# Softmax denominators from node blocks added on VectorE, and feed-forward blocks spread over the attention quads, in a two-layer graph kernel

## The chip, the cores and the metric

One core of one Trainium2 chip. The metric is the device time of one execution in microseconds (us), the median of several runs on the same chip. A trace of one execution accompanies every kernel. The engines are TensorE (PE in the profile, its weight loads PEld), VectorE (DVE), ScalarE (ACT), GpSimd (POOL) and the sync engine (SP).

## The reference, cut to what matters

64 graphs of 256 nodes with 256 features pass a graph attention layer (two attentions, a feed-forward block of width 1024) and then a relational attention layer with 8 heads of 32 features and 4 relations. The adjacency is 0 or 1, so only relations 0 and 1 occur. The change is in the second layer's attention:

```python
scores = jnp.einsum('bhid,bhjd->bhij', q, k) / np.sqrt(dh)
attn = jax.nn.softmax(scores, axis=-1)
out = jnp.zeros_like(q)
for r in range(Wv.shape[0]):
    v_r = (src @ Wv[r] + bv[r]).reshape(Bb, Nn, h, dh).transpose(0, 2, 1, 3)
    mask = (adj_matrix == r)[:, None]
    out = out + jnp.einsum('bhij,bhjd->bhid', attn * mask, v_r)
```

## The kernel before

Everything is float32. Graphs go two at a time (a group; 32 groups). A turn of the software pipeline works on three groups at once: the second layer of group `y_`, the rest of the first layer of `x_ = y_ + 1`, and the first attention of `z = y_ + 2`. TensorE's order is fixed by hand, to the order in which the code issues its instructions. The last turns, 30 and 31, lack a `z`, and turn 31 lacks an `x_` too.

The attention of a group is four quads: graph `b` (2) by half of the heads `m` (2, four heads each). `weighted` computes the transposed scores, their exponentials `e` (no maximum is subtracted; a check at the end guards this) and `ea = e * adjacency`. `applied` sums over the source nodes, which lie on the partitions in two blocks `j` of 128: `zo`, the denominators, by products with ones; `po`, the numerators, by products with the values (relation 0 for all, the difference of relations 1 and 0 where the adjacency is 1). Each head has 32 output columns, so four heads lie beside each other in TensorE as column tiles (128*32 in the trace). `divided` ends a graph. (`P` is 128, `N` 256, `NB` 2, `HPB` 4, `DH` 32, `F` 256.)

```python
    def weighted(u, b, m, q, k_, aT):
        ...                                  # scores: 8 products into four of six rotating PSUM banks
        for a in range(HPB):
            nc.scalar.activation(e[:, a, :], ps[a], AF.Exp, scale=isd)
        for a in range(0, HPB, 2):
            nc.vector.tensor_tensor(ea[:, a:a + 2, :], e[:, a:a + 2, :],
                                    ab[:, None, :].to_broadcast([P, 2, NB * N]), ALU.mult)
        return e, ea

    def applied(b, m, v, e, ea, po, zo):
        terms = [(zo, lambda h, j: ones, e), (po, lambda h, j: v[:, b * NB + j, h * DH:(h + 1) * DH], e),
                 (po, lambda h, j: v[:, b * NB + j, F + h * DH:F + (h + 1) * DH], ea)]
        for n, (to, lhs, rhs) in enumerate(terms):
            for j in range(NB):
                for a in range(HPB):
                    hp = slice(a * DH, (a + 1) * DH)
                    nc.tensor.matmul(to[hp, m * N:(m + 1) * N], lhs(m * HPB + a, j),
                                     rhs[:, a, j * N:(j + 1) * N],
                                     start=(n < 2 and j == 0), stop=(n != 1 and j == NB - 1))

    def divided(u, b, po, zo, oT):
        rz = work.tile([P, KB * N], F32, tag="rz", name=f"rz{u}_{b}")
        nc.vector.reciprocal(rz, zo)
        nc.gpsimd.tensor_add(low, low, rz)
        nc.vector.tensor_tensor(oT[...], po..., rz..., ALU.mult)
    ...
    def turn(y_, x_, z):
        ...                                  # values, queries, keys; then the attention stretch:
            e = {0: weighted(y_, *quads[0], q, k_, aT)}
        ...
            h1 = hidden(x_, 0, h1hT, wf1, bf1, AF.Relu, range(FB // 2))
        ...
            e[1] = weighted(y_, *quads[1], q, k_, aT)
            apply_(0)
            e[2] = weighted(y_, *quads[2], q, k_, aT)
            apply_(1)
            e[3] = weighted(y_, *quads[3], q, k_, aT)
        ...
            hidden(x_, 0, h1hT, wf1, bf1, AF.Relu, range(FB // 2, FB), h1)
        ...
            early(z)                         # transposes of adjacency (aTp) and input (xT)
        ...
            apply_(2)
            apply_(3)
        ...                                  # out_(0), project(z), out_(1): yop, xpp, yop
```

## Time and profile before

| | before |
|---|---|
| median of 3 runs | 3420.71 us (3419.79 to 3422.26) |
| TensorE, VectorE, ScalarE, GpSimd busy | 98%, 49%, 32%, 29% |
| granted TensorE clock, mean | 0.991 |
| steady turn (first aTp to the next first aTp) | 103.64 us |

A busy share says which engine to look at, not what an instruction costs. In this document a stretch of TensorE lasts from the first start of one group of instructions to the first start of the next group, because the lengths given for matmuls overlap (rows of 1.05 us start 0.86 us apart). The prediction shows the lines.

### The profile page before, as it was taken

What the parts mean: (1) busy time and instruction counts of PE and PEld (TensorE: products, weight loads), DVE (VectorE), ACT (ScalarE), POOL (GpSimd) and SP (SyncE); (2) the same over time, 40 slices, a digit from 0 to 9 for tenths busy, and PEclk for the clock granted to TensorE, in tenths of its full rate; (3) what the DMA queues carried; (4) which work ended last, traced back from release to release, by engine and by line L of the source; (5) the groups of instructions that cost most, each with busy time, mean ns of one, the idle gap of its engine ahead of it and who ended that gap; (6) DMA issues with size and microseconds to landing.
All of it is one profiled execution on the core that took longest, in us unless ns stands there. A gap on an engine that the chain in (4) does not pass through costs nothing.

```text
span 3419.7 us, 45212 instructions
## 1 busy us (share of the span) xinstructions
PE 3341.6 (98%) x18970; PEld 2199.3 (64%) x18970; DVE 1683.3 (49%) x3479; ACT 1079.6 (32%) x1920; POOL 983.7 (29%) x844
## 2 busy tenths in 40 slices
PE   4899999999999999999999999999999999999997
PEld 3566666666666666666666666676666666666664
DVE  2545555444554444554454554454544445554544
ACT  1333323323323323333333333233233233333222
POOL 1233232332322332322332323322323323223312
PEclk8999999999999999999999999999999999999998
DMA  4000000000000000000000000000000000000000
GB/s 122 17 15 14 13 19 19 13 19 7 19 19 19 13 19 7 19 19 19 13 19 7 20 19 13 19 10 16 20 19 13 19 7 20 19 19 7 7 1 14
DMA packets 62465, 61.04 MB, mean 18 GB/s; under 512 B 7216, under 2 KB 61616, under 8 KB 62256
## 3 DMA queue, kind: packets, MB, share of 16 engines
q1 hardware_dynamic: 33792, 33.56, 3.0%
q0 software_dynamic: 16896, 16.78, 2.1%
q10 hardware_dynamic: 11568, 7.76, 0.9%
q8 instruction: 151, 2.47, 0.3%
q14 instruction: 58, 0.48, 0.0%
HBM read 41.31 MB, written 16.78 MB: 17 GB/s over the span
## 4 chain that ended last, share of the span: by engine, by line
PE 97%; DVE 1%; DMA 1%; ACTq 0%; POOL 0%; issue 0%; ACT 0%; POOLq 0%; DVEq 0%
PE h1p L655 26%; PE yfp L617 26%; PE vp L687 6%; PE po L723 6%; PE sp L703 4%; PE zo L723 4%; PE hpp L606 3%; PE yop L617 3%; PE kp L674 3%; PE qp L674 3%; PE ygp L617 3%; PE xpp L568 3%; PE rows L578 1%; PE aTp L555 1%; DMA b<-in_L_gnn_b_dram 0%; ACTq L462 0%
## 5 line engine op out<-in xcount | busy, mean ns | idle before, releaser
L655 PE MATMUL h1p<-h1T,wf 128*128 128x512 f32 x1024 | 457.5, 600 | 0.1
L711 DVE TENSOR_TENSOR ea<-e,aT 128x1024 f32<-128x1024 f32 x256 | 317.9, 1283 | 272.7 <-ACT e L709 272.7
L655 PE MATMUL h1p<-h3T,w 128*128 128x512 f32 x1024 | 446.5, 594 | 1.4 <-DVE h3T L544 1.4
L617 PE MATMUL yfp<-wf,h 128*128 128x256 f32 x2048 | 447.3, 379 | 0.0
L617 PE MATMUL yfp<-w,h 128*128 128x256 f32 x2048 | 447.3, 379 | 0.0
L617 PEld LDWEIGHTS yfp<-w,h 128*128 128x128 f32 x2048 | 386.8, 190 | 52.2 <-issue 1.0
L617 PEld LDWEIGHTS yfp<-wf,h 128*128 128x128 f32 x2048 | 386.7, 190 | 51.3
L709 ACT ACTIVATE e<-sp 128x512 f32<-128x512 f32 x512 | 264.2, 604 | 380.3 <-PE sp L703 380.3
L655 PEld LDWEIGHTS h1p<-h3T,w 128*128 128x128 f32 x1024 | 194.8, 191 | 234.3 <-issue 229.4
L655 PEld LDWEIGHTS h1p<-h1T,wf 128*128 128x128 f32 x1024 | 189.8, 190 | 236.5 <-issue 217.8
L730 POOL TENSOR_TENSOR low<-low,rz 128x512 f32<-128x512 f32 x64 | 81.1, 1268 | 852.4 <-DVE rz L729 852.4
L587 DVE SCALAR_TENSOR_TENSOR s<-s 128x512 f32<-128x512 f32 x128 | 90.3, 706 | 443.0 <-ACT s L584 441.8
L645 POOL TENSOR_TENSOR res<-res,rb 128x1024 f32<-128x1024 f32 x128 | 301.1, 2352 | 10.0
L620 DVE TENSOR_TENSOR yf<-yfp,res 128x512 f32<-128x512 f32 x128 | 88.5, 692 | 424.7 <-PE yfp L617 423.4
L633 POOL TENSOR_TENSOR rs<-ve,mhalf 128x4 f32<-128x4 f32 x128 | 130.6, 1020 | 456.5 <-DVE ve L632 456.5
L657 ACT ACTIVATE h<-h1p,b 128x512 f32<-128x512 f32 x256 | 175.8, 687 | 250.7 <-PE h1p L655 249.4
L729 DVE RECIPROCAL rz<-zo 128x512 f32<-128x512 f32 x64 | 214.7, 3354 | 67.5 <-PE zo L723 67.5
L657 ACT ACTIVATE h<-h1p,bf 128x512 f32<-128x512 f32 x256 | 176.9, 691 | 213.9 <-PE h1p L655 213.9
L687 PE MATMUL vp<-wv,h2T 128*128 128x512 f32 x512 | 230.1, 592 | 0.0
L676 ACT ACTIVATE q<-qp,bq 128x512 f32<-128x512 f32 x64 | 44.0, 687 | 530.6 <-PE qp L674 530.6
L608 ACT COPY hp<-hpp 128x258 f32<-128x258 f32 x128 | 47.9, 374 | 442.5 <-PE hpp L606 442.5
L644 POOL TENSOR_TENSOR res<-yf,rg 128x1024 f32<-128x1024 f32 x64 | 150.5, 2351 | 95.8 <-DVE yf L637 94.3
(485 smaller groups left out, 4319.7 us busy)
## 6 DMA issues: line engine op xcount, KB each, us to landing
xs<-in_x_dram SPq DMA_DIRECT2D x32, 512.0 KB, 3.8
af<-in_adj_dram POOLq DMA_DIRECT2D x32, 512.0 KB, 4.4
out_dram<-res SPq DMA_DIRECT2D x32, 512.0 KB, 2.9
wf<-in_L_gnn_w_ff_dram ACTq DMA_DIRECT2D x2, 1024.0 KB, 11.5
w<-in_L_gnn_W_dram ACTq DMA_DIRECT2D x2, 1024.0 KB, 10.0
wv<-in_L_gnn_Wv_dram ACTq DMA_DIRECT2D x2, 256.0 KB, 4.6
gw<-in_L_gnn_W_dram ACTq DMA_DIRECT2D x1, 256.0 KB, 4.5
gw2e<-in_L_gnn_W_dram ACTq DMA_DIRECT2D x1, 256.0 KB, 6.9
```

The lines of the kernel that those rows point to most:

```text
L617: nc.tensor.matmul(ps[:, i * F:(i + 1) * F], lhs(t, k), rhs(b, k), start=(k == 0), stop=(k == n - 1))
L644: nc.gpsimd.tensor_mul(r, xn, g[:, None, :].to_broadcast([P, T, F]))
L645: nc.gpsimd.tensor_add(r, r, b[:, None, :].to_broadcast([P, T, F]))
L655: nc.tensor.matmul(ps, wi[:, k, f * P:(f + 1) * P], hT[:, k, :], start=(k == 0), stop=(k == KB - 1))
L657: nc.scalar.activation(h1[:, f, :], ps, func, bias=bi[:, f:f + 1])
L674: nc.tensor.matmul(ps, w[:, k, m * P:(m + 1) * P], hT[:, k, :], start=(k == 0), stop=(k == KB - 1))
L687: nc.tensor.matmul(ps, hT[:, k, t * P:(t + 1) * P], wvf[:, k, :], start=(k == 0), stop=(k == KB - 1))
L703: nc.tensor.matmul(ps[a][:, j * N:(j + 1) * N], k_[hp, m, j0:j0 + P], q[hp, m, b * N:(b + 1) * N], start=True, stop=True)
L709: nc.scalar.activation(e[:, a, :], ps[a], AF.Exp, scale=isd)
L711: nc.vector.tensor_tensor(ea[:, a:a + 2, :], e[:, a:a + 2, :], ab[:, None, :].to_broadcast([P, 2, NB * N]), ALU.mult)
L723: nc.tensor.matmul(to[hp, m * N:(m + 1) * N], lhs(m * HPB + a, j), rhs[:, a, j * N:(j + 1) * N], start=(n < 2 and j == 0), stop=(n != 1 an ...
L729: nc.vector.reciprocal(rz, zo)
```

## The change

Its intent: TensorE is the bound, and half of the zo products only add two blocks of nodes. VectorE, half idle, can add the blocks, and then one product with ones a head is enough. The sums take VectorE time between the scores and the apply of a quad, so the eight hidden blocks of the other group's feed-forward are spread to give it that time. The diff, with cuts:

```diff
-        return e, ea
+        es = work.tile([P, HPB, N], F32, tag="es", name=f"es{n}")
+        nc.vector.tensor_add(es, e[:, :, 0:N], e[:, :, N:2 * N])
+        return e, ea, es
...
+        terms = [(j, v[:, b * NB + j, r * F + m * P:r * F + (m + 1) * P], w)
+                 for r, w in ((0, e), (1, ea)) for j in range(NB)]
+        for n, (j, vs, w) in enumerate(terms):
+            for a in range(HPB):
+                hp = slice(a * DH, (a + 1) * DH)
+                nc.tensor.matmul(po[hp, m * N:(m + 1) * N], vs[:, hp], w[:, a, j * N:(j + 1) * N],
+                                 start=(n == 0), stop=(n == len(terms) - 1))
+        for a in range(HPB):
+            nc.tensor.matmul(zo[a * DH:(a + 1) * DH, m * N:(m + 1) * N], ones, es[:, a, :],
+                             start=True, stop=True)
...
+            if have(y_):
+                yield scores, 0
+            yield hid, range(0, 3)
+            if have(y_):
+                yield scores, 1
+                yield apply_, 0
+            yield hid, range(3, 4)
+            if have(y_):
+                yield scores, 2
+                yield apply_, 1
+            yield hid, range(4, 6)
+            if have(y_):
+                yield scores, 3
+            yield hid, range(6, 8)
+            if have(z):
+                yield early, z
+            if have(y_):
+                yield apply_, 2
+                yield apply_, 3
```

Three things change, then: half of zo goes, four sums a turn come, and the hidden blocks stand at four places instead of two. A fourth: zo is now the last term of an apply, and was the first.

More of the change, by code (lines that the diff above doesn't have):

```diff
@@ L712, in weighted, with applied @@
                                     ab[:, None, :].to_broadcast([P, 2, NB * N]), ALU.mult)
-        return e, ea
-    def applied(b, m, v, e, ea, po, zo):
-        terms = [(zo, lambda h, j: ones, e), (po, lambda h, j: v[:, b * NB + j, h * DH:(h + 1) * DH], e),
-                 (po, lambda h, j: v[:, b * NB + j, F + h * DH:F + (h + 1) * DH], ea)]
-        for n, (to, lhs, rhs) in enumerate(terms):
-            for j in range(NB):
-                for a in range(HPB):
-                    hp = slice(a * DH, (a + 1) * DH)
-                    nc.tensor.matmul(to[hp, m * N:(m + 1) * N], lhs(m * HPB + a, j),
-                                     rhs[:, a, j * N:(j + 1) * N],
-                                     start=(n < 2 and j == 0), stop=(n != 1 and j == NB - 1))
+        es = work.tile([P, HPB, N], F32, tag="es", name=f"es{n}")
+        nc.vector.tensor_add(es, e[:, :, 0:N], e[:, :, N:2 * N])
+        return e, ea, es
+    def applied(b, m, v, e, ea, es, po, zo):
+        terms = [(j, v[:, b * NB + j, r * F + m * P:r * F + (m + 1) * P], w)
[8 more added lines that the diff above has]
+                             start=True, stop=True)
     def divided(u, b, po, zo, oT):
@@ L790, in turn, with scores @@
             acc = [None] * G
-            e = {0: weighted(y_, *quads[0], q, k_, aT)}
+            e = {}
+            def scores(n):
+                e[n] = weighted(y_, *quads[n], q, k_, aT)
             def apply_(n):
@@ L799, in apply_, with steps, hid @@
                     divided(y_, b, *acc[b], oT)
-        if have(x_):
-            h1 = hidden(x_, 0, h1hT, wf1, bf1, AF.Relu, range(FB // 2))
-        if have(y_):
-            e[1] = weighted(y_, *quads[1], q, k_, aT)
-            apply_(0)
-            e[2] = weighted(y_, *quads[2], q, k_, aT)
-            apply_(1)
-            e[3] = weighted(y_, *quads[3], q, k_, aT)
-        if have(x_):
-            hidden(x_, 0, h1hT, wf1, bf1, AF.Relu, range(FB // 2, FB), h1)
-        if have(z):
-            early(z)
-        if have(y_):
-            apply_(2)
-            apply_(3)
+        h1 = None
+        def steps():
+            if have(y_):
[17 more added lines that the diff above has]
+                yield apply_, 3
+        def hid(blocks):
+            nonlocal h1
+            if have(x_):
+                h1 = hidden(x_, 0, h1hT, wf1, bf1, AF.Relu, blocks, h1)
+        for do, what in steps():
+            do(what)
         if have(y_):
```

## The prediction

> **What bounds the kernel now.** I read the page's busy shares and slices first, then the chain that ended last, then the timeline of one turn of the software pipeline on TensorE, VectorE and ScalarE, and last the groups by shape.
>
> The page: busy time, the TensorE slices, the chain.
>
> ```profile
> PE 3341.6 (98%) x18970; PEld 2199.3 (64%) x18970; DVE 1683.3 (49%) x3479; ACT 1079.6 (32%) x1920; POOL 983.7 (29%) x844
> ...
> PE   4899999999999999999999999999999999999997
> ...
> PE 97%; DVE 1%; DMA 1%; ACTq 0%; POOL 0%; issue 0%; ACT 0%; POOLq 0%; DVEq 0%
> ```
>
> TensorE is busy 98% and the chain that ended last is TensorE for 97% of the span; only the first 5% and the last slice have holes. A microsecond off another engine is worth nothing unless TensorE waits for it. So the question is how many microseconds of TensorE issue go and come. A busy share cannot tell that (ends of matmuls are modelled, durations overlap), so I take differences of starts from the timeline of TensorE: start, length, engine, line, operation, tiles, count.
>
> ```profile
> 1545.42 13.90 PE L655 MATMUL h1p<-h3T,w 128*128 128x512 f32 x32
> 1559.15 0.60 PE L578 MATMUL rows<-ident,hp 128*128 128x128 f32 x4
> ...
> 1592.43 1.15 PE L703 MATMUL sp<-q,k 32*128 32x256 f32 x16
> 1593.51 7.13 PE L655 MATMUL h1p<-h1T,wf 128*128 128x512 f32 x16
> 1600.57 1.15 PE L703 MATMUL sp<-q,k 32*128 32x256 f32 x16
> 1601.65 1.07 PE L723 MATMUL zo<-e,ones 128*32 128x256 f32 x16
> 1602.54 1.05 PE L723 MATMUL po<-e,v 128*32 128x256 f32 x16
> 1603.40 1.05 PE L723 MATMUL po<-ea,v 128*32 128x256 f32 x16
> 1604.38 1.15 PE L703 MATMUL sp<-q,k 32*128 32x256 f32 x16
> ...
> 1609.26 7.13 PE L655 MATMUL h1p<-h1T,wf 128*128 128x512 f32 x16
> 1616.23 1.04 PE L555 MATMUL aTp<-ident,af 128*128 128x128 f32 x8
> ...
> 1622.41 1.05 PE L723 MATMUL po<-ea,v 128*32 128x256 f32 x16
> 1623.38 0.92 PE L617 MATMUL yop<-wo,oT 128*128 128x256 f32 x3
> ```
>
> No row has an idle time in brackets: in a steady turn TensorE waits for nobody. Turns repeat exactly; the first aTp of this turn starts at 1616.23 and that of the turn before at 1512.59, 103.64 us apart. Each product in the source is two instructions here (8 products in a zo term, 16 instructions).
>
> VectorE and ScalarE of the same turn show when their results are ready:
>
> ```profile
> 1594.71 2.36 DVE L711 TENSOR_TENSOR ea<-e,aT 128x1024 f32<-128x1024 f32 x2 [1.48 <-ACT e L709]
> 1602.85 2.36 DVE L711 TENSOR_TENSOR ea<-e,aT 128x1024 f32<-128x1024 f32 x2 [5.78 <-ACT e L709]
> 1606.65 2.36 DVE L711 TENSOR_TENSOR ea<-e,aT 128x1024 f32<-128x1024 f32 x2 [1.44 <-ACT e L709]
> 1608.93 3.35 DVE L729 RECIPROCAL rz<-zo 128x512 f32<-128x512 f32 x1
> 1612.39 0.69 DVE L731 TENSOR_TENSOR oT<-po,rz 128x512 f32<-128x512 f32 x1
> 1613.00 2.85 DVE L711 TENSOR_TENSOR ea<-e,aT 128x1024 f32<-128x1024 f32 x2
> ```
>
> VectorE waits for ScalarE's exponentials here, not the other way round. From 1592.4 to 1623.4 (the attention stretch, 31.0 us) it is busy 18.54 us, so it has room.
>
> [...] rows of 1.05 us start 0.86 us apart; hence starts only. [...] This kernel has three modes: full array (128*128), four row tiles (scores, 32*128), four column tiles (zo and po, 128*32). The plain rate of a full 512-column instruction is 13.73/32 = 0.429 us (h1p on h3T), so 16 take 6.87. Between two score groups 16 took 7.06 (1593.51 to 1600.57), between scores and transposes 6.97 (1609.26 to 1616.23): entering full from row mode costs 0.10, leaving it for row mode 0.09. A po term followed by po lasts 0.86; followed by scores 0.98, by yop 0.97: leaving column mode costs 0.11 to 0.12. [...] the same-sized ea products take 1222 ns in the stretch 1592 to 1610 (grouped by shape), 1283 over the run. [...] the ea pair of 2.85 us instead of 2.36 ran beside GpSimd's addition to low[...].
>
> **The change part by part.**
>
> (1) The zo term is halved. Before: 2 node blocks by 4 heads = 8 products a quad; after: 4, on e already added over the blocks. Four column tiles run together: 16 instructions start over 0.86 us (po) to 0.89 (zo, the term after scores), so 8 cost 0.43. Four quads a turn: 1.73 us; 32 turns: 55 us, all on TensorE and all on the path. That is 1.6% of 3421 at the very most.
>
> (2) The node blocks are added on VectorE: four more 128x1024 additions a turn, about 1.22 each by ea, 4.9 us; 128 of them are 156 us, VectorE rises from 1683 to some 1840 us (54%). In the attention stretch 18.5 becomes 23.4 of about 29.6 us. Off the path if no wait follows; checked under the clock below.
>
> (3) The hidden blocks, before as 4 behind scores 0 and 4 behind scores 3, become 3, 1, 2, 2. The products are the same, but two groups now stand between an apply and the next scores. Before, column to row: 0.11. After, column to full 0.11, entry to full 0.10, full to row 0.09. Net 0.20 for each of two places: 0.39 us a turn. Since TensorE had no wait to fill, spreading buys nothing of itself; it only makes room for the additions.
>
> (4) zo moves to the end of an apply. It is the same mode as po, so no switch. But the reciprocal (3.35) and oT (0.69) of a batch start about 1.7 us later relative to the end of the products.
>
> Steady turn: -1.73 + 0.39 = -1.34, from 103.64 to 102.30.
>
> **A clock of the new stretch** (estimate from the durations above; 0 is the first scores): scores 0 to 1.08; 3 blocks to 6.42; scores 1 to 7.50; apply 0 (0.89 + 0.86 + 0.43 + 0.11) to 9.79; 1 block to 11.70; scores 2 to 12.78; apply 1 to 15.07; 2 blocks to 18.70; scores 3 to 19.77; 2 blocks to 23.31; transposes to 25.15; apply 2 to 27.33; apply 3 to 29.60 (30.95 before). VectorE starts ea 2.28 after its scores: quad 0 has its sum at 5.9 (zo wants it at 9.3); quad 1 at 12.3 (wanted 14.5); quad 2 at 17.6; then rz and oT of batch 0 to 21.7 (apply 2 wants the banks at 25.15); ea and sum of quad 3 to 25.8 (wanted 28 and 29); the adjacency check and the xT copies to 28.3 (wanted 31.4). Then rz from about 29.75, oT ready at 33.9; the second yop, behind the first (1.83) and the projection (3.51), wants it at 34.9. Every wait is covered, the last by only 1.0 us (it was 2.8).
>
> The ends: turn 30 has no following group, so no projection stands between the yops. Before, the second yop already waited 0.6 there; zo coming last adds about 2.0, so this turn gains nothing and loses 0.7. Turn 31 has no hidden blocks, and TensorE waited there 3.02 for rz: three sums go ahead of that rz (3.6 us), less what TensorE saves, and the last rz starts later: some 2.3 us longer. Sum: 30 x -1.34 + 0.7 + 2.3 = -37; 3420.7 - 37 = 3384.
>
> **Rivals.** Rival A, mode switches free: 55 - 3 saved, 3369. Against it: 7.06 beside 6.97 and 6.87. Rival B, VectorE late for the second yop: the covering 1.0 us is the smallest, the scheduler may put other VectorE work ahead of the last rz[...]. One us late in 30 turns gives 3415, two 3445. For it: the small cover; against it: VectorE has over 6 us of slack in the stretch, and the queue is empty before that rz on my clock. Rival C, the spread blocks feed TensorE that was starved, and more than 55 us comes back: against it, no bracketed idle in any steady turn. Rival D, six rotating PSUM banks: scores take four at once and now alternate with blocks; a late evacuation would hold scores, perhaps 0.5 us at two places, 3415. Against it: ScalarE empties a block in 0.69 us against 1.72 of its products, and is 32% busy.
>
> **Range and chances.** Middle 3384; low end 3372 (switches half as dear, ends free); high end 3403 (a stall of 0.6 a turn). Faster by 2% would be under 3352, more than the whole zo saving can give: 0.02. Slower by 2% is over 3489, a stall of more than 3 us in every turn: 0.02. Within 2%: 0.96.
>
> **What would show it.** Right: aTp to aTp 102.3 us in steady turns; zo terms of 8 instructions starting over 0.43; hidden groups of 12, 4, 8, 8 instructions each 0.2 over 0.429 apiece; no bracketed idle on scores, zo, po and yop between turns 0 and 29; es sums near 1.22. Wrong: a wait of yop for oT or of zo for es in every turn (rival B), of sp for ACT (rival D), or a po to h1p to sp passage that costs no more than po to sp (rival A).

The 1.22 us of a sum rests on the ea products, which have its size (128x1024; 1222 ns). One of rival B's reasons, a stretching of VectorE's work by GpSimd, was not shown; the trace shows no more than an ea pair of 2.85 us instead of 2.36 that ran partly beside GpSimd's addition.

## The result, and the profile after

The changed kernel took 3389.39 us (median of 6 runs, 3388.31 to 3390.61) where the kernel before took 3421.24 (6 runs). The ratio is 0.9907, with a 95% interval of 0.9895 to 0.9920. Ratios here come from the runs of both kernels in the same rounds, and differ from the ratio of the medians quoted by up to 0.0004. The kernel before ran beside every experiment on the same chip; its medians there were 3420.8 to 3422.3 us.

The page of the changed kernel, busy shares:

```profile
PE 3304.7 (98%) x17946; PEld 2164.6 (64%) x17946; DVE 1820.3 (54%) x3607; ACT 1083.8 (32%) x1920; POOL 986.0 (29%) x844
```

TensorE lost 1024 matmul instructions and 37 us, VectorE gained 128 instructions and 137 us, and TensorE is as full as it was. TensorE's timeline of one steady attention stretch:

```profile
1573.75 1.15 PE L703 MATMUL sp<-q,k 32*128 32x256 f32 x16
1574.83 5.42 PE L655 MATMUL h1p<-h1T,wf 128*128 128x512 f32 x12
1580.18 1.15 PE L703 MATMUL sp<-q,k 32*128 32x256 f32 x16
1581.25 1.07 PE L724 MATMUL po<-e,v 128*32 128x256 f32 x16
1582.14 1.05 PE L724 MATMUL po<-ea,v 128*32 128x256 f32 x16
1583.00 0.61 PE L727 MATMUL zo<-es,ones 128*32 128x256 f32 x8
1583.55 1.98 PE L655 MATMUL h1p<-h1T,wf 128*128 128x512 f32 x4
1585.46 1.15 PE L703 MATMUL sp<-q,k 32*128 32x256 f32 x16
...
1601.96 1.05 PE L724 MATMUL po<-ea,v 128*32 128x256 f32 x16
1602.83 0.61 PE L727 MATMUL zo<-es,ones 128*32 128x256 f32 x8
1603.37 1.99 PE L617 MATMUL yop<-wo,oT 128*128 128x256 f32 x8
1605.20 3.67 PE L568 MATMUL xpp<-gwe,xT 128*128 128x260 f32 x16
1608.71 1.89 PE L617 MATMUL yop<-wo,oT 128*128 128x256 f32 x8
```

No row waits. A zo term now lasts 0.43 us plus the 0.11 for leaving column mode (1583.00 to 1583.55), where it lasted 0.86 to 0.89. And the single hidden block lasts 1.91 us (1583.55 to 1585.46) for 4 instructions that take 1.72 at the plain rate of 0.429: the 0.20 that a group pays for standing between an apply and scores. From scores 0 to the first yop it is 29.62 us (1573.75 to 1603.37), before 30.95. Every turn from 1 to 29 lasts 102.31 us, before 103.64.

VectorE at the end of that stretch:

```profile
1603.51 3.36 DVE L732 RECIPROCAL rz<-zo 128x512 f32<-128x512 f32 x1 [1.91 <-PE zo L727]
1606.78 0.63 DVE L620 TENSOR_TENSOR yo<-yop,res 128x512 f32<-128x512 f32 x1
1607.33 0.68 DVE L734 TENSOR_TENSOR oT<-po,rz 128x512 f32<-128x512 f32 x1
```

VectorE waits 1.91 us for zo, so all sums are done in time. oT is ready at 1608.01 and the second yop starts at 1608.71: 0.7 us of cover are left.

The gain of a steady turn, 1.33 us, over 30 turns is 40 us. The kernel gained 32 by the medians, 31 between the two traces. The rest went at the end. To see where, compare turn 31 in both traces. TensorE before:

```profile
3354.11 1.15 PE L703 MATMUL sp<-q,k 32*128 32x256 f32 x16
3358.27 1.94 PE L723 MATMUL zo<-e,ones 128*32 128x256 f32 x16 [3.02 <-DVE rz L729]
3359.98 1.53 PE L723 MATMUL po<-e,v 128*32 128x256 f32 x16
...
3367.52 1.99 PE L617 MATMUL yop<-wo,oT 128*128 128x256 f32 x8 [0.64 <-DVE oT L731]
...
3375.26 15.36 PE L655 MATMUL h1p<-h3T,w 128*128 128x512 f32 x32 [0.43 <-DVE h3T L544]
```

TensorE after:

```profile
3314.84 1.15 PE L703 MATMUL sp<-q,k 32*128 32x256 f32 x16
3322.71 1.94 PE L724 MATMUL po<-e,v 128*32 128x256 f32 x16 [6.72 <-DVE oT L734]
3324.39 1.97 PE L724 MATMUL po<-ea,v 128*32 128x256 f32 x16
...
3333.98 3.63 PE L617 MATMUL yop<-wo,oT 128*128 128x256 f32 x8 [2.69 <-DVE oT L734]
...
3343.50 16.01 PE L655 MATMUL h1p<-h3T,w 128*128 128x512 f32 x32
```

There is no hidden block in this turn to hide anything behind. Apply 2 waits 6.72 us where it waited 3.02, the second yop 2.69 where it waited 0.64. The brackets also name another releaser for apply 2: before, it began with zo and needed only rz; now it begins with po and needs oT, the division after rz. And the po term after the pause lasts 1.68 us (3322.71 to 3324.39) instead of 0.86. The stretches of the changed kernel with the granted clock show why. The columns are the window, its length, the busy us of TensorE, its weight loads, VectorE, ScalarE and GpSimd, the granted TensorE clock, the DMA share and the GB/s moved:

```profile
3308.00:3315.00 7.00, 6.92 (x106) 3.23 (x105) 7.00 (x7) 4.29 (x9) 0.00 (x0) 1.00 0.01 2
3315.00:3322.70 7.70, 0.99 (x16) 0.58 (x17) 7.70 (x7) 3.35 (x5) 1.73 (x1) 0.84 0.00 1
3322.70:3326.90 4.20, 4.19 (x40) 2.27 (x44) 2.60 (x2) 0.00 (x0) 0.39 (x1) 0.50 0.00 0
```

The clock is 1.00 before the pause and 0.50 after it. So a pause of 6.7 us was followed by about 4 us at half rate. A shorter pause was too: in the kernel before, zo took 1.71 us (3358.27 to 3359.98, granted clock 0.50) after a wait of 3.02. In the clock records of the traces before and after the change every half-clock stretch but the last, which the end cuts off, lasts 3.41 us or a whole multiple of it (3.41 to 27.31). The prediction did not reckon with this.

From here on a turn is measured from the first yfp of the second feed-forward to the next such yfp, which covers all turns. The parts of the difference of the spans (3388.5 less 3419.7):

| part | before | after | difference |
|---|---|---|---|
| start, with turn 0 (to the first such yfp) | 212.26 | 210.89 | -1.37 |
| turns 1 to 29, each | 103.64 | 102.31 | -1.33 (-38.6 in all) |
| turn 30 | 96.40 | 97.20 | +0.80 |
| turn 31 | 76.22 | 84.29 | +8.07 |
| after it | 29.20 | 29.19 | 0 |

### The profile page after: what moved, and what is told of

Its sections match the earlier page's. It is cut to its first block, busy times and chain, and to the rows that moved or that the text cites. A ratio compares the mean times of both kernels' runs of the same rounds, so it can differ in the third digit from the quotient of the medians.

```text
span 3388.5 us, 43264 instructions
## 1 busy us (share of the span) xinstructions
PE 3304.7 (98%) x17946; PEld 2164.6 (64%) x17946; DVE 1820.3 (54%) x3607; ACT 1083.8 (32%) x1920; POOL 986.0 (29%) x844
## 4 chain that ended last, share of the span: by engine, by line
PE 96%; DVE 1%; ACTq 1%; DMA 0%; issue 0%; POOL 0%; ACT 0%; POOLq 0%; DVEq 0%
PE h1p L655 27%; PE yfp L617 26%; PE po L724 7%; PE vp L687 6%; PE sp L703 4%; PE yop L617 3%; PE hpp L606 3%; PE kp L674 3%; PE ygp L617 3%; PE qp L674 3%; PE xpp L568 3%; PE zo L727 2%; PE rows L578 1%; PE aTp L555 1%; ACTq L462 1%
## 5 line engine op out<-in xcount | busy, mean ns | idle before, releaser
L655 PE MATMUL h1p<-h1T,wf 128*128 128x512 f32 x1024 | 474.6, 607 | 0.1
```

The costliest lines, as they stand in the source:

```text
L655: nc.tensor.matmul(ps, wi[:, k, f * P:(f + 1) * P], hT[:, k, :], start=(k == 0), stop=(k == KB - 1))
```

## The experiments

My theory: TensorE's issue time and its mode switches set the steady turn; halving zo gives 1.73 us, spreading costs 0.39, the sums lie beside; the ends pay for late reciprocals. The main rivals: spreading is what makes the halving possible, and the sums cost something in steady turns. The turns of each trace and the medians, with the ratio to the kernel before in the same rounds:

| run | steady turn | turn 30 | turn 31 | median us | ratio |
|---|---|---|---|---|---|
| before | 103.64 | 96.40 | 76.22 | 3421.24 | 1 |
| the change | 102.31 | 97.20 | 84.29 | 3389.39 | 0.9907 |
| halved, not spread | 101.91 | 98.49 | 84.34 | 3379.47 | 0.9876 |
| spread only | 104.04 | 96.79 | 77.35 | 3436.28 | 1.0037 |
| zo last only | 103.64 | 98.53 | 84.09 | 3431.42 | 1.0026 |
| no sum (wrong result) | 102.31 | 97.20 | 78.60 | 3386.09 | 0.9893 |
| old form in the last turn | 102.31 | 97.20 | 77.31 | 3382.87 | 0.9886 |
| warm last turn | 102.31 | 97.20 | 78.34 | 3384.21 | 0.9891 |
| not spread, old form at the end | 101.91 | 96.40 | 76.68 | 3369.11 | 0.9849 |
| the same, more banks | 101.91 | 96.40 | 74.25 | 3367.85 | 0.9842 |
| two sums, not spread | 102.99 | 100.30 | 87.66 | 3416.95 | 0.9983 |
| two sums, spread | 102.31 | 99.25 | 83.25 | 3392.84 | 0.9914 |
| not spread, old form at the end, warm | 101.91 | 96.39 | 73.55 | 3368.78 | 0.9841 |

The steady turns repeat to a hundredth of a us within a trace. The stretch up to the first such yfp, in which the first transfers arrive, lasted 209.8 to 214.9 us over these traces with no pattern that I found, so differences of 2 or 3 us are judged by turns and not by whole runs.

### Halved, not spread

```diff
-            yield hid, range(0, 3)
+            yield hid, range(0, 4)
             scores 1, apply 0
-            yield hid, range(3, 4)
             scores 2, apply 1
-            yield hid, range(4, 6)
             scores 3
-            yield hid, range(6, 8)
+            yield hid, range(4, 8)
```

> The denominators halved as in the change, the hidden blocks left where they were before (four behind scores 0, four behind scores 3). My theory (TensorE issue time plus mode switches sets the turn): the saving of 1.73 us a turn stays whole and the two extra mode rounds of 0.20 us are gone, so a steady turn lasts 103.64 - 1.73 = 101.91 us against 102.31 in the changed kernel, and the run is 30 x 0.40 = 12 us shorter than it, about 3377 us. Rival (the spreading is what makes room for VectorE's sums): without it zo waits for es in quad 1 (my estimate leaves it 0.3 us) or the second yop waits for oT, bracketed idle appears on TensorE in every turn, and the steady turn is 102.3 us or longer, the run 3389 us or more.

Measured: 101.91 us a steady turn, and no row of TensorE waits in it; 3379.47 us, ratio 0.9876 (0.9860 to 0.9891). For the steady turn the theory holds to the hundredth, and the rival falls: one sum a quad needs no spreading here. Spreading cost 0.40 us a turn, 11.6 us over turns 1 to 29. The run gained only 10, 2.5 us less than expected, as turn 30 took 98.49 us and not 97.20: after its wait of 2.79 us the second yop ran at half clock (3.41 us, 3230.79 to 3234.20). In the changed kernel the same wait of 2.79 us was followed by a yop at full clock (1.80 us, 3243.35 to 3245.15).

### Spread only

The spread order with `weighted` and `applied` of the kernel before (no `es`, zo over both blocks, first).

> The hidden blocks spread as in the change, denominators as before (16 zo instructions a quad, no sum on VectorE). Theory: only the two extra mode rounds are added, 0.39 us a turn, steady turn 104.03 us, the run 12 us longer than before, about 3433 us. Rival (spreading costs nothing or feeds a starved TensorE): steady turn 103.64 us or less, 3421 us or less.

Measured: 104.04 us a steady turn, 0.40 more than before; 3436.28 us, ratio 1.0037 (1.0024 to 1.0051). The run is 3 us over what was expected; its start took 2.7 us longer than that of before, of which only 0.4 are the change's. Spreading alone is a loss, as TensorE had no pause to fill.

### zo last only

```diff
-        terms = [(zo, ones, e), (po, v0, e), (po, v1, ea)]
+        terms = [(po, v0, e), (po, v1, ea), (zo, ones, e)]
```

(The terms are abbreviated; the start and stop flags follow.)

> The kernel before with one edit: the zo term comes last in an apply and not first; no sum, no spreading. Theory: same mode, so the steady turn stays 103.64 us; the reciprocal starts 1.7 us later, which costs about 2 us in turn 30 (second yop waits for oT) and 2 to 4 us in turn 31, the last: run about 3425 us. Rival (the late end of the changed kernel comes from the sums alone): no difference from before, 3421 us.

Measured: steady turn 103.64, turn 30 2.1 longer, as expected; but turn 31 is 7.87 us longer, not 2 to 4, and the run took 3431.42. The order of terms alone costs as much at the end as the whole change. The pause ahead of apply 2 grew by only 1.8 us (scores 3 to apply 2: 4.16 before, 5.92 here). That growth is not a later reciprocal: rz starts 0.75 us after scores 3, before 0.76. It is the new releaser: po needs oT, and VectorE puts one ea product between rz (3358.89) and oT (3363.24), so po starts at 3364.07. Ahead of the second yop the wait grew from 0.64 to 2.69. The rest is slow work after pauses: three whole terms at 1.7 us instead of 0.86.

### No sum

```diff
-        es = work.tile([P, HPB, N], F32, tag="es", name=f"es{n}")
-        nc.vector.tensor_add(es, e[:, :, 0:N], e[:, :, N:2 * N])
-        return e, ea, es
+        return e, ea, e[:, :, 0:N]
```

> Wrong result on purpose: the changed kernel with zo taken from the first node block of e alone, so TensorE does exactly what it does in the changed kernel and VectorE's 128 sums are gone. Theory: the sums lie beside TensorE in every steady turn, which stays 102.31 us; only turn 31 shortens, by about 3.4 us or more (three sums stood ahead of the first reciprocal there), so about 3385 us. Rival (the sums cost TensorE time in steady turns[...]): the steady turn falls below 102.31 us and the run falls by more than 10 us.

Measured, with a wrong result: steady turn 102.31, the same to the hundredth; turn 31 at 78.60 instead of 84.29; 3386.09 us. So the 128 sums cost nothing in the steady turns and 5.7 us in the last. Only 1.5 us of that is wait ahead of apply 2 (6.72 less 5.21). The rest, 4.2 us, goes with the clock: 17.07 us of turn 31 are at half clock in the change, 6.83 here, and the 10.24 us between them can cost up to half their length (an estimate from the po term: 1.68 us at clock 0.50, 0.86 at 1.00).

### Old form in the last turn

```diff
+        if u == NG - 1:
+            return e, ea, None       # applied: zo first, over both blocks, where es is None
         es = work.tile([P, HPB, N], F32, tag="es", name=f"es{n}")
```

The halved clock that the expectation names is that of the changed kernel above: 0.50 from 3322.7 to 3326.9, after the pause of 6.72 us.

> The changed kernel, but in the last turn (31) alone the denominators are taken in the old form: zo first, over both node blocks, no sum. Theory (the 8 us lost at the end are the three sums ahead of the first reciprocal, the later zo, and the halved TensorE clock that follows the longer pauses): steady turns stay 102.31 us, turn 31 (from its first yfp of the second feed-forward to the next) comes back from 84.3 to 76 to 77.5 us, the run from 3389 to about 3382 us. Rival (the lost time at the end belongs to the spreading or to something else in the change): turn 31 stays above 82 us.

Measured: turn 31 at 77.31, the rest unchanged, 3382.87 us. The last turn's loss belongs to the late zo and the sums, not to the spreading. The 1.1 us over the 76.22 of the kernel before go with the clock: TensorE's waits in the attention are the same (3.01 and 0.63 us), but 10.24 us of the turn are at half clock instead of 6.83.

### Warm last turn

```diff
+        def filler(n):
+            for _ in range(n):
+                ps = bank("fill")
+                nc.tensor.matmul(ps, wf2[:, 0, 0:P], wf1[:, 0, 0:512], start=True, stop=True)
...
+            if y_ == NG - 1: filler(7)       # ahead of apply 2
+        if y_ == NG - 1: filler(2)           # ahead of out_(1)
+        if y_ == NG - 1: filler(3)           # ahead of h3T
```

> The changed kernel with products that nobody reads put into TensorE's pauses of the last turn: 14 instructions ahead of apply 2, 4 ahead of the second yop, 6 ahead of the transposes of h3T; nothing is taken from VectorE's chain. Theory that the pauses also halve the clock afterwards: the waits for oT end at the same time, but po after the pause starts 0.87 us per 16 instructions and not 1.68, the first hidden group of h3T takes about 13.8 and not 15.8 us, the granted clock of that stretch is 1.00, and turn 31 takes about 78 us instead of 84.3, the run about 3383 us. Rival (only the lengths of the waits matter, the slow products come from their operands): turn 31 stays 84 us or becomes longer.

Measured: turn 31 at 78.34 instead of 84.29, 3384.21 us. TensorE's timeline of this kernel in turn 31:

```profile
3315.80 6.28 PE L812 MATMUL fill<-wf,wf 128*128 128x512 f32 x14
3322.49 1.07 PE L724 MATMUL po<-e,v 128*32 128x256 f32 x16 [0.42 <-DVE oT L734]
3323.38 1.05 PE L724 MATMUL po<-ea,v 128*32 128x256 f32 x16
```

Its stretches, columns as above:

```profile
3314.70:3322.50 7.80, 7.38 (x35) 3.31 (x31) 7.80 (x7) 3.35 (x5) 1.65 (x1) 1.00 0.00 1
3322.50:3326.90 4.40, 4.40 (x80) 2.49 (x80) 2.69 (x2) 0.00 (x0) 0.48 (x1) 1.00 0.02 4
```

Apply 2 starts 7.77 us after scores 3 (7.87 without the fillers), so nothing was taken from the wait. But the po term lasts 0.89 instead of 1.68, the hidden group of h3T 13.84 instead of 15.84, and the clock is 1.00 in the whole turn. Work that nobody reads made the turn 5.95 us shorter. The rival, that only the waits matter, falls.

### Not spread, old form at the end

The not-spread order, and turns 30 and 31 in the old form (`if u >= NG - 2: return e, ea, None`).

> Denominators halved, hidden blocks not spread, and turns 30 and 31 in the old form (zo first, both blocks, no sum). Theory: steady turns 101.91 us as in the run without spreading; turn 30 back from 98.5 to 96.4 us; turn 31 back from 84.3 to 76 to 77.5 us: about 9 to 10 us under the run without spreading, some 3370 us, ratio to before about 0.985. Rival: the ends are not additive, 3375 us or more.

Measured: 101.91, 96.40 and 76.68 us; 3369.11 us, ratio 0.9849 (0.9836 to 0.9863), correct. The parts add up. It beats the kernel before and the change.

### The same with more banks

```diff
+                    if y_ == NG - 1 and b == 1:
+                        acc[b] = [bank(f"{t_}{y_}_{b}") for t_ in ("po", "zo")]
+                    else:
                         acc[b] = [psum.tile(...) for t_ in ("po", "zo")]
```

> As the run before it in this list, and in turn 31 batch 1 takes its po and zo from the rotating banks, so apply 2 need not wait until batch 0 is divided. Theory: the 3 us wait of apply 2 for oT is gone, apply 3 now waits for ea, which stands behind batch 0's reciprocal on VectorE, and the last reciprocal starts 1.5 us earlier: 1.5 to 3 us under the run before it, about 3368 us. Rival: VectorE's order is the bound of that turn and nothing is gained.

Measured: turn 31 at 74.25, 2.4 us less; apply 2 follows scores 3 after 1.08 us, and instead the ea term of apply 3 waits for VectorE (brackets of 1.01 and 0.51 us). Not all of the 2.4 is the shorter wait: 3.41 us of the turn are at half clock instead of 6.83, worth some 1.5 us (an estimate: half the time that TensorE was busy at half clock, 6.42 and 3.36 us). 3367.85 us, ratio 0.9842 (0.9829 to 0.9856): by whole runs not distinguishable from the run before it.

### Two sums, not spread; two sums, spread

```diff
         nc.vector.tensor_add(es, e[:, :, 0:N], e[:, :, N:2 * N])
+        nc.vector.tensor_add(es, e[:, :, 0:N], e[:, :, N:2 * N])
```

> Every sum of node blocks done twice (the second writes the same values), hidden blocks not spread. Theory (the spread blocks are a cushion for VectorE that one sum doesn't need): in quad 1 the second sum ends about 0.9 us after zo wants it, so zo waits for es in every steady turn, which lasts about 102.8 us instead of 101.91; run about 3405 us. Rival (VectorE has room anywhere): no bracketed idle, 101.91 us, about 3382 us.

> Every sum done twice, hidden blocks spread as in the changed kernel. Theory: the cushion takes the second sum too, at most a few tenths of a us of wait at the second yop; steady turn 102.3 to 102.6 us, so the order turns round and spreading wins by 0.2 to 0.5 us a turn; run about 3395 us. Rival: the second sums push the last reciprocal of each turn past the second yop by 1 us or more, steady turn over 103.3 us.

Measured: not spread 102.99 us a steady turn and 3416.95 us; spread 102.31 and 3392.84 us. The not-spread kernel's timeline:

```profile
1596.92 1.05 PE L725 MATMUL po<-ea,v 128*32 128x256 f32 x16
1598.67 0.64 PE L728 MATMUL zo<-es,ones 128*32 128x256 f32 x8 [0.71 <-DVE es L715]
```

zo of quad 1 waits for its sum, as reckoned: its start slips by 0.89 us (1596.92 to 1598.67 is 1.75 where a po term takes 0.86). The turn lost 1.08 us against one sum; the other 0.2 are small delays at zo itself, the projection and the second yop. I had expected 0.9 of it, and the run ended 12 us above my figure, as turns 30 and 31 grew by 1.8 and 3.3 too. The spread kernel takes the second sum with no wait at all. So the spreading does what it was meant for, only one sum is too little to need it: with two, it wins by 0.68 us a turn; with one, it loses 0.40.

### Not spread, old form at the end, warm

The kernel of two sections above without the extra banks, with 3 unread products ahead of apply 2 and 3 ahead of h3T in turn 31.

> The not-spread kernel with the old form in turns 30 and 31, and unread products in two pauses of turn 31 (6 instructions ahead of apply 2, 6 ahead of the transposes of h3T). Theory: the clock stays at 1.00, po after the pause is 0.87 per 16, the hidden group of h3T 13.8 instead of 15.4, turn 31 about 73.5 us instead of 76.7; run about 3366 us. Rival: the fillers delay what follows them by as much as the clock gives, 3369 us.

Measured: turn 31 at 73.55 as expected (76.68 without), the hidden group 13.84; the clock is 1.00 in the whole turn; but 3368.78 us for the run, as its start took 212.7 us in the trace where that of the run without took 209.8. The gain is seen in the turn and lost in the spread of the starts.

## Why the prediction was right

The predicted time was 3384 us, the measured 3389.4, inside 3372 to 3403, and within the 2% to which the prediction gave a chance of 0.96. Point by point:

- **zo halved, -1.73 us a turn.** Right: without spreading the turn fell by exactly 1.73 (103.64 to 101.91).
- **Spreading, +0.39.** Right: 0.40 alone (104.04) and 0.40 on top of the halving. The sign to look for, hidden groups "each 0.2 over 0.429 apiece", held for the groups of 12, 4 and 8 (5.35, 1.91, 3.63 us); the last group, which goes to transposes and not to scores, pays 0.10, as the prediction's own clock had it.
- **Sums beside TensorE.** Right: removing them left the turn at 102.31. They last 1.217 us each (predicted 1.22). VectorE's busy time rose by 137 us and not by 156, mostly because a sum overlaps the ends of its neighbours: the next instruction starts 1.13 us after it (1590.07 to 1591.20 in quad 2).
- **The smallest cover, at the second yop.** Right in kind: 0.7 us, predicted 1.0. VectorE took yo of the first yop (0.55 us) between rz and oT, which the clock had left out.
- **Rivals.** A (switches free) is out by the 0.40; B and D (waits for oT, banks) did not occur in a steady turn; C (a starved TensorE) is out by the spread-only run.
- **Turn 30, +0.7.** Right: +0.80, with the second yop waiting 2.79 instead of 0.63. But luck helped: the run without spreading had the same wait, and its clock halved after it, which cost 1.7 us more (98.49 where its shorter steady turn leads to 96.8). The prediction had no such cost.
- **Turn 31, +2.3.** Wrong in size: +8.07. This is the term that failed. Two causes share it. With unread products filling the pauses, which removes the clock's part, the old form takes 73.55 and the changed one 78.34: 4.8 us are the waits themselves, twice what was predicted. The clock costs 2.7 us in the old form (76.22 less 73.55) and 5.95 in the changed one, so its part in the change is 3.3 us. The brackets of the traces show where the waits came from. Ahead of apply 2: 3.02 us before, 4.78 with zo last alone, 5.21 without the sums, 6.72 in the change; ahead of the second yop 0.64 before and 2.69 in the other three. Of the 5.75 us of added wait (more than the 4.8, as the halved zo takes work off TensorE too) the late zo brings 3.8, the sums 1.5 and the halving 0.4. The prediction had reckoned 3.6 us of sums ahead of rz; it did not see that apply 2 would wait for oT instead of rz. What each of these pauses cost by the clock stays open: it doesn't follow the length of the wait (half clock for 17.07 us of the turn with 4.78 us ahead of apply 2, for 6.83 with 5.21).

The miss is 5.8 us in one of 32 turns, so it left the total in its range.

## What to carry to other kernels

When one engine is full and repeats exactly, count its starts: a removed product is worth its start-to-start time (here 32 instructions a turn, 1.73 us), and a group moved between groups of another tiling mode costs its switches, here 0.20 us each. Spread work only where a trace shows a wait for it to fill; the same spreading lost 0.40 us a turn with one sum and won 0.68 with two. Treat the last turns of a pipeline apart: what hides VectorE work is missing there (turn 31 grew by 8.07 us here), and a pause of TensorE of a few us can be paid twice, by its length and by the half clock after it (here a wait of 6.72 us, then clock 0.50 and a po term of 1.68 us instead of 0.86). Whether it is can't be told from the length alone: of two waits of 2.79 us one was followed by half clock and the other was not. Products that nobody reads, put into such pauses, took 5.95 us off a turn of 84.29 here.
